# A two-layer image block on one core: how the constants come in, and which engines fold the weights, in its first microseconds

## The chip, the core and the metric

The kernel runs on one core of a Trainium2 chip. A core has five engines that run side by side, each through its own list of instructions in order: TensorE (PE in the profile; its weight loads are PEld), VectorE (DVE), ScalarE (ACT), GpSimd (POOL) and SyncE (SP), which here only starts transfers. Transfers are carried out by 16 DMA engines; an engine that starts one puts it into its own DMA queue. The metric is the device time of one execution in microseconds (us).

## What is computed

The input x is four images of 128 channels by 128 by 128 pixels, in float32. Two layers follow each other, each with a residual:

```
gn(v)    : normalize groups of 4 channels over the whole image
layer 0  : x = x + block(gn(x)) + block(gn(x) transposed, and back)
block(t) : per pixel, over the 128 channels
           t   = ln(t; ln0)
           t   = t + silu(ln(t; ln1)) @ W_out^T
           w   = ln(t; ln2) @ W_whiten^T
           t   = t + sigmoid(w @ W_recep^T) * (relu(w @ W_key^T)^2 @ W_value^T)
layer 1  : x = x + conv3x3(gn(x)) (+ bias), scaled by a gate from channel means
```

The block acts on each pixel by itself, so both calls of layer 0 give the same and the kernel computes it once and counts it twice. Two points matter for what follows. First, gn(x) needs mean and variance of a whole image before its first pixel can be normalized. Second, no nonlinearity stands between W_whiten and W_key or W_recep, so the kernel multiplies these weights with each other once at the start, together with gain and bias of ln2 and with the subtraction of the mean over channels ("folding"). In the loop there is one product with wk_s and bias kbias, and one with wr_s and rbias.

## The kernel before

Channels lie on the 128 partitions. An image is cut into 8 blocks of 16 rows (1 MB each, tiles x) and 32 chunks of 512 pixels; two chunks are a pair, 64 pairs in all. Work on the pairs is software-pipelined: lists of words (FILL, FIRST, ORDER, HANDOVER, END) say by hand, operation by operation, in which order the engines get the steps of different pairs. FILL starts the pipeline; FIRST repeats for image 0 alone; later orders mix in the convolution of layer 1 for the image before. In this hand-ordered part (from line 1010) the order is as written. Before it the scheduler of the tile framework sets the order on each engine; a buffer that is reused is waited for, and so is what an instruction reads.

What comes before the hand-ordered part is what the change touches:

- `load_block` (L284) starts one transfer of a block of x; L292 calls it for the 8 blocks of image 0. The transfers are issued by SP (L287).
- ident, gmat, nhalf and mean_of (L296 to L315) are constants that GpSimd makes. mean_of has 1/128 everywhere.
- `load_const` (L317) issues transfers of constants from ScalarE (L319). `column` (L322) brings a vector of 128 numbers in as a column, one number on each partition: g1, b1, g2, b2, cb. g0 and b0 are read 128 times over, so that each partition holds the whole vector. wo, wv, s1, s2 are weights.
- `times_root` (L325) multiplies the three gains with the square root of 128 on VectorE (L326).
- ww, wkt, wrt (L353) hold W_whiten, W_key and W_recep until they are folded; ScalarE issues them too (L354 to L356).
- The folding loop (L357 to L369) runs twice, for the key weights (512 columns) and the receptance weights (128). TensorE multiplies (pw, L359); VectorE copies to raw (L361) and scales by g2 to raw2 (L362); TensorE makes the column means with mean_of (pc, L364); VectorE subtracts them (L365, into wk_s or wr_s); TensorE multiplies raw with b2 (pb, L368); VectorE copies the bias (L369). L371 halves rbias.
- `in_stats` (L890) takes the statistics of one chunk on VectorE (L894, 32 times for image 0). `input_norm` (L401) runs `group_norm` (L377): VectorE aggregates (mv, L380), TensorE averages over groups (pm L383, pv L391), GpSimd takes the root (L394), and VectorE makes nb (L404).
- Only with nb can `lay` (u, L588, ScalarE) normalize the first chunk, and FILL go on: u is transposed on TensorE (ut), gets its statistics (L601), is normalized to t (L577), and so on.
- `fetch_stats` (L884) loads half-block pieces of later images into a ring of one buffer (xs, L888), for their statistics; SP issues these as well.

Matmul outputs with the tag "h" share two PSUM banks; SBUF tiles with the tag "h" share six buffers, and "y", "y2" and "r" two each.

Of the kernel before, what the change touches and what calls it, by code (L numbers as in the profile page):

```python
# [9 lines left out]
F32 = mybir.dt.float32  # L10
AF = mybir.ActivationFunctionType
ALU = mybir.AluOpType

P = 128
# [3 lines left out]
BLK_ROWS = 16  # L18
# [196 lines left out]
def conv_preact_kernel(  # L215
# [40 lines left out]
    nc = tc.nc  # L256
    B, C, H, W = x.shape
    HID = w_key_t.shape[1]
    NH = HID // P
    NSE = se_w1_t.shape[1]  # L260
    BLK = BLK_ROWS * W
    NBLK = H // BLK_ROWS
# [7 lines left out]
    const = ctx.enter_context(tc.tile_pool(name="const", bufs=1))  # L270
    xp = ctx.enter_context(tc.tile_pool(name="xp", bufs=12))
    wg = ctx.enter_context(tc.tile_pool(name="wg", bufs=4))
    wk = ctx.enter_context(tc.tile_pool(name="wk", bufs=2))
# [5 lines left out]
    def bank(tag, name, bufs=2):  # L279
        return ps.tile([P, CH], F32, tag=tag, name=name, bufs=bufs)  # L280

    blocks = {}

    def load_block(g):  # L284
        b, k = g // NBLK, g % NBLK
        blocks[g] = xp.tile([P, BLK], F32, tag="x", name=f"x_{b}_{k}")
        nc.sync.dma_start(  # L287
            blocks[g],
            x[b, :, k * BLK_ROWS : (k + 1) * BLK_ROWS, :].rearrange("c h w -> c (h w)"),
        )  # L290

    for g in range(NBLK):  # L292
        load_block(g)


    ident = const.tile([P, P], F32, tag="ident", name="ident")  # L296
# [14 lines left out]

    nhalf = const.tile([P, N], F32, tag="nhalf", name="nhalf")
    nc.gpsimd.memset(nhalf, -0.5)
    mean_of = const.tile([P, P], F32, tag="mean_of", name="mean_of")
    nc.gpsimd.memset(mean_of, 1.0 / C)  # L315

    def load_const(name, src, shape):  # L317
        t = const.tile(shape, F32, tag=name, name=name)
        nc.scalar.dma_start(t, src)  # L319
        return t  # L320

    def column(name, src):  # L322
        return load_const(name, src.rearrange("(c o) -> c o", o=1), [P, 1])

    def times_root(t):  # L325
        nc.vector.tensor_scalar(t, t, C**0.5, None, ALU.mult)  # L326

    g1 = column("g1", ln1_g)
    b1 = column("b1", ln1_b)
    g2 = column("g2", ln2_g)  # L330
    b2 = column("b2", ln2_b)
    cb = column("cb", conv_b)
    g0 = load_const("g0", ln0_g.rearrange("(o c) -> o c", o=1).to_broadcast([P, C]), [P, C])
    b0 = load_const("b0", ln0_b.rearrange("(o c) -> o c", o=1).to_broadcast([P, C]), [P, C])
    for gain_of in (g0, g1, g2):
        times_root(gain_of)
    wo = load_const("wo", w_out_t, [P, P])
    wv = load_const("wv", w_value_t.rearrange("(j p) c -> p j c", p=P), [P, NH, P])
    s1 = load_const("s1", se_w1_t, [P, NSE])
    s2 = load_const("s2", se_w2_t, [NSE, P])  # L340

# [1 line left out]
    wk_s = const.tile([P, HID], F32, tag="wk_s", name="wk_s")  # L345
    wr_s = const.tile([P, P], F32, tag="wr_s", name="wr_s")
    kbias = const.tile([P, NH], F32, tag="kbias", name="kbias")
    rbias = const.tile([P, 1], F32, tag="rbias", name="rbias")

    def staged(name, n):  # L350
        return wk.tile([P, n], F32, tag="h", name=name, bufs=6)

    ww, wkt, wrt = staged("ww", P), staged("wkt", HID), staged("wrt", P)  # L353
    nc.scalar.dma_start(ww, w_whiten)  # L354
    nc.scalar.dma_start(wkt, w_key_t)
    nc.scalar.dma_start(wrt, w_recep_t)  # L356
    for src, n, dst, bias in ((wkt, HID, wk_s, kbias), (wrt, P, wr_s, rbias)):  # L357
        pw = bank("h", "pw")
        nc.tensor.matmul(pw[:, :n], ww, src, start=True, stop=True)  # L359
        raw, raw2 = staged("raw", n), staged("raw2", HID)  # L360
        nc.vector.tensor_copy(raw, pw[:, :n])  # L361
        nc.vector.tensor_scalar(raw2[:, :n], raw, g2, None, ALU.mult)  # L362
        pc = bank("h", "pc")
        nc.tensor.matmul(pc[:, :n], mean_of, raw2[:, :n], start=True, stop=True)  # L364
        nc.vector.tensor_tensor(dst, raw2[:, :n], pc[:, :n], ALU.subtract)  # L365
        pb = bank("h", "pb")
        for j in range(n // P):
            nc.tensor.matmul(pb[:, j : j + 1], raw[:, ts(j, P)], b2, start=True, stop=True)  # L368
        nc.vector.tensor_copy(bias, pb[:, : n // P])  # L369

    nc.vector.tensor_scalar(rbias, rbias, 0.5, None, ALU.mult)  # L371


    def col(name):
# [585 lines left out]
    def slot(s, order):  # L960
# [6 lines left out]
        if s % 2 and s + 1 >= NP and len(blocks) < B * NBLK:  # L967
            load_block(len(blocks))
# [26 lines left out]
    def work_off(chain, words, block, pair):  # L995
        for op, n in words:
            if op == "*":
                next(chain, None)
            elif op == "load":
                load_block(len(blocks))  # L1000
            elif op == "fetch":
                fetch_stats(n)
            elif op in ("in0", "in1"):
                in_stats(n, int(op[2]), S["in", n][:, ts(int(op[2]), CH)])
            elif op in EVEN or op in ODD:
                conv_op(op, block(n))
            else:
                layer0_op(op, pair(n))
# [52 lines left out]
```

## Time and profile before

| | |
|---|---|
| median of 8 runs | 1903.68 us (1900.76 to 1907.06) |
| the profiled execution | 1899.84 us |
| its span in the profile | 1898.0 us |
| statistics of image 0 (L894 on x) | 32, mean 681 ns, first at 9.4, last from 37.8 us |
| first instruction of ScalarE on pixels (u, L588) | 42.68 us |
| transfers from ScalarE's queue in the first 40 us | 2288 packets, 0.87 MB |
| transfers from SP's queue in the first 40 us | 1296 packets, 8.91 MB |
| read from HBM, whole run | 97.27 MB |

The profile is one execution, and its span begins with the first instruction. Busy shares on the page are means over the whole span. In a list in order of time, the columns are start, duration, engine, line of the code, operation, tile written and tile read, shape, and the count of instructions merged; in brackets stands how long the engine had stood idle before, and what ended that. A window's row gives, after its length, the busy time of the five engine columns with the count of instructions, the granted clock of TensorE, the share of time in which the 16 DMA engines were busy, and the rate in GB/s.

### The profile page before, as it was taken

Reading aid. Unit: us, or ns where it says so; the run is one execution under the profiler, and the core shown is the slowest. Engines: PE = TensorE matmul, PEld = TensorE weight load, DVE = VectorE, ACT = ScalarE, POOL = GpSimd, SP = SyncE. Lnnn points to the kernel's source line nnn. Section 1 sums busy time; section 2 is a strip of 40 time slices with the busy share of each in tenths; the row PEclk is TensorE's granted clock in tenths of the full one; section 3 lists DMA queues with packets and bytes.
Section 4 is the critical chain, followed back from the end, with each engine's and each line's share of the span. In section 5 each row is a group of like instructions: output and inputs, shape, how many; then the busy total and the mean of one; then the engine's idle time right before and its main releaser. Section 6 shows DMA issues by size and latency. Waiting matters only on the chain.

```text
span 1898.0 us, 21640 instructions
## 1 busy us (share of the span) xinstructions
PE 1810.6 (95%) x6154; PEld 942.7 (50%) x6154; DVE 1359.3 (72%) x3348; ACT 1271.4 (67%) x2478; POOL 1156.8 (61%) x1913
## 2 busy tenths in 40 slices
PE   2699999999999999998999999999999999999998
PEld 1455555555455555454555455455455555554443
DVE  5766776677677677677777677667676667666987
ACT  0789988898667676776777776676577777753000
POOL 0877887897356665665676666666566677631211
PEclk9999999999999999999999999999999999999999
DMA  5311111311122212213222212112111211111112
GB/s 206 89 46 56 56 46 45 124 59 56 56 78 89 89 67 78 78 55 105 72 84 90 69 47 86 67 56 80 47 45 67 67 57 67 49 38 42 53 67 89
DMA packets 41880, 133.68 MB, mean 70 GB/s; under 512 B 5776, under 2 KB 10912, under 8 KB 33568
## 3 DMA queue, kind: packets, MB, share of 16 engines
q1 hardware_dynamic: 39472, 131.42, 19.7%
q10 hardware_dynamic: 2288, 0.87, 0.3%
q8 instruction: 49, 0.80, 0.2%
q14 instruction: 71, 0.58, 0.1%
HBM read 97.27 MB, written 35.00 MB: 70 GB/s over the span
## 4 chain that ended last, share of the span: by engine, by line
PE 84%; DVE 4%; ACT 3%; POOL 3%; issue 1%; DMA 0%; POOLq 0%; DVEq 0%; ACTq 0%
PE kv L735 21%; PE pk L708 21%; PE m L773 8%; PE m L775 8%; PE m L774 8%; PE pr L726 5%; PE att L669 5%; PE tt L570 3%; PE z1t L570 2%; PE ut L570 2%; POOL rs L624 1%; ACT t L577 1%; DVE st L601 1%; ACT z L577 1%; DVE v L797 1%
## 5 line engine op out<-in xcount | busy, mean ns | idle before, releaser
L708 PE MATMUL pk<-y,wk_s 128*128 128x512 f32 x1024 | 500.1, 595 | 7.0 <-DVE y L697 5.6
L735 PE MATMUL kv<-h,wv 128*128 128x512 f32 x1024 | 487.1, 593 | 0.0
L712 ACT ACTIVATE h<-pk,kbias 128x512 f32<-128x512 f32 x512 | 349.9, 686 | 172.0 <-PE pk L708 165.6
L624 POOL TENSOR_TENSOR rs<-rs,nhalf 128x8 f32<-128x8 f32 x192 | 317.4, 1653 | 12.1 <-DVE rs L617 6.0
L735 PEld LDWEIGHTS kv<-h,wv 128*128 128x128 f32 x1024 | 185.9, 190 | 207.5 <-issue 185.8
L718 ACT ACTIVATE h<-h 128x512 f32<-128x512 f32 x480 | 284.5, 630 | 4.2
L708 PEld LDWEIGHTS pk<-y,wk_s 128*128 128x128 f32 x1024 | 182.5, 190 | 195.4 <-issue 146.0
L755 POOL TENSOR_TENSOR x<-x,r 128x512 f32<-128x512 f32 x128 | 164.4, 1285 | 187.8 <-DVE r L751 178.5
L577 ACT ACTIVATE t<-ut,nb,rs 128x128 f32<-128x128 f32 x512 | 191.6, 464 | 125.2 <-POOL nb L631 114.7
L601 DVE BATCH_NORM_STATS2 st<-t 128x6 f32<-128x128 f32 x1024 | 219.5, 276 | 22.1 <-POOL t L652 19.6
L577 ACT ACTIVATE z<-t,nb,rs 128x128 f32<-128x128 f32 x512 | 210.0, 487 | 13.6 <-POOL nb L631 12.8
L648 POOL TENSOR_TENSOR t<-t,g 128x512 f32<-128x512 f32 x128 | 162.9, 1278 | 73.9 <-ACT t L577 73.8
L773 PE MATMUL m<-v,u 128*128 128x512 f32 x384 | 198.8, 599 | 6.7 <-ACT e L849 3.6
L774 PE MATMUL m<-v,u 128*128 128x508 f32 x384 | 194.9, 589 | 0.0
L775 PE MATMUL m<-v,u 128*128 128x508 f32 x384 | 194.9, 589 | 0.0
L613 POOL TENSOR_TENSOR rs<-st 128x8 f32<-128x8 f32 x186 | 57.1, 307 | 210.0 <-DVE st L601 208.4
L652 POOL TENSOR_TENSOR t<-t,b 128x512 f32<-128x512 f32 x128 | 164.0, 1287 | 6.7
L669 PEld LDWEIGHTS att<-wo,y 128*128 128x128 f32 x1024 | 131.1, 196 | 26.2 <-issue 17.8
L601 DVE BATCH_NORM_STATS2 st<-ut 128x6 f32<-128x128 f32 x512 | 112.4, 284 | 41.2 <-PE ut L570 41.2
L730 ACT ACTIVATE r<-pr,rbias 128x512 f32<-128x512 f32 x128 | 87.6, 684 | 80.0 <-PE pr L726 64.7
L669 PE MATMUL att<-wo,y 128*128 128x128 f32 x1024 | 138.4, 280 | 2.2 <-ACT y L663 1.6
L726 PE MATMUL pr<-y,wr_s 128*128 128x512 f32 x256 | 131.7, 597 | 3.2 <-ACT h L712 2.5
(144 smaller groups left out, 2437.3 us busy)
## 6 DMA issues: line engine op xcount, KB each, us to landing
x<-in_x SPq DMA_DIRECT2D x32, 1024.0 KB
R<-rd SPq DMA_DIRECT2D x128, 256.0 KB
out<-x SPq DMA_DIRECT2D x32, 1024.0 KB
xs<-in_x SPq DMA_DIRECT2D x48, 512.0 KB
u<-raw SPq DMA_DIRECT2D x18, 192.0 KB
raw<-u SPq DMA_DIRECT2D x6, 192.0 KB
rd<-rrow SPq DMA_DIRECT2D x64, 4.0 KB
u_w<-in_conv_w SPq DMA_DIRECT2D x3, 192.0 KB
```

The costliest lines, as they stand in the source:

```text
L577: nc.scalar.activation(dst[:, s, :], src[:, s, :], AF.Identity, bias=nb[:, i : i + 1], scale=rs[:, i : i + 1],)
L601: nc.vector.bn_stats(st[:, h * SUB + s, :], src[:, s, :])
L624: nc.gpsimd.tensor_tensor(rs, rs, nhalf, ALU.pow)
L669: nc.tensor.matmul(att[:, ts(s, P)], y[:, ts(s, P)], wo, start=True, stop=True)
L708: nc.tensor.matmul(pk, wk_s[:, ts(j, P)], S["y2", g, h], start=True, stop=True)
L712: nc.scalar.activation(k, S["pk", g, h, j], AF.Relu, bias=kbias[:, j : j + 1])
L718: nc.scalar.activation(k, k, AF.Square)
L726: nc.tensor.matmul(pr, wr_s, S["y2", g, h], start=True, stop=True)
L735: nc.tensor.matmul(S["kv", g, h], wv[:, j, :], S.pop(("h", g, h, j)), start=(j == 0), stop=(j == NH - 1))
L773: nc.tensor.matmul(pc, u[:, 1], v, start=True, stop=False)
L774: nc.tensor.matmul(pc[:, :, 1:W], u[:, 0], v[:, :, 0 : W - 1], start=False, stop=False)
L775: nc.tensor.matmul(pc[:, :, 0 : W - 1], u[:, 2], v[:, :, 1:W], start=False, stop=True)
```

## The change

- Block 7 of image 0, the last of the first eight, is loaded in two halves.
- All constants are issued by SP, in one queue with x, in this order: blocks 0 to 3; the five vectors ln1_g, ln1_b, ln2_g, ln2_b and conv_b as five rows of one tile (vec); ln0_g and ln0_b as one row each; ww, wkt, wrt; blocks 4 to 7; wo, wv, s1, s2.
- The five rows become columns by one matmul with the identity (pv), the two rows are spread over the partitions by a matmul with a row of ones (pr). ScalarE copies them from PSUM and multiplies the gains by the square root of 128 on the way.
- In the folding, ScalarE takes over all that VectorE did. mean_of is replaced by centre, the identity minus 1/128, so that the matmul gives the centred weights and no subtraction is left. The factor 0.5 of rbias is applied with its copy.
- VectorE keeps the statistics alone.

The rest of the kernel, the hand-ordered lists among it, is the same. The core of the diff:

```diff
     def load_block(g):
         b, k = g // NBLK, g % NBLK
         blocks[g] = xp.tile([P, BLK], F32, tag="x", name=f"x_{b}_{k}")
-        nc.sync.dma_start(
-            blocks[g],
-            x[b, :, k * BLK_ROWS : (k + 1) * BLK_ROWS, :].rearrange("c h w -> c (h w)"),
-        )
-
-    for g in range(NBLK):
+        parts = 2 if g == NBLK - 1 else 1
+        R = BLK_ROWS // parts
+        for i in range(parts):
+            r = k * BLK_ROWS + i * R
+            nc.sync.dma_start(
+                blocks[g][:, i * R * W : (i + 1) * R * W],
+                x[b, :, r : r + R, :].rearrange("c h w -> c (h w)"),
+            )
+
+    def load_const(name, src, shape, pool=const, tag=None):
+        t = pool.tile(shape, F32, tag=tag or name, name=name)
+        nc.sync.dma_start(t, src)
+        return t
+
+    def staged(name, n, src=None):
+        t = wk.tile([P, n], F32, tag="h", name=name, bufs=6)
+        if src is not None:
+            nc.sync.dma_start(t, src)
+        return t
+
+    for g in range(NBLK // 2):
         load_block(g)
+    vec = wk.tile([5, C], F32, tag="y", name="vec")
+    for i, src in enumerate((ln1_g, ln1_b, ln2_g, ln2_b, conv_b)):
+        nc.sync.dma_start(vec[i : i + 1, :], src.rearrange("(o c) -> o c", o=1))
+    row0 = [
+        load_const(n, src.rearrange("(o c) -> o c", o=1), [1, C], wk, "y2")
+        for n, src in (("g0row", ln0_g), ("b0row", ln0_b))
+    ]
+    ww, wkt = staged("ww", P, w_whiten), staged("wkt", HID, w_key_t)
+    wrt = staged("wrt", P, w_recep_t)
+    for g in range(NBLK // 2, NBLK):
+        load_block(g)
+    wo = load_const("wo", w_out_t, [P, P])
+    wv = load_const("wv", w_value_t.rearrange("(j p) c -> p j c", p=P), [P, NH, P])
+    s1 = load_const("s1", se_w1_t, [P, NSE])
+    s2 = load_const("s2", se_w2_t, [NSE, P])
...
-    mean_of = const.tile([P, P], F32, tag="mean_of", name="mean_of")
-    nc.gpsimd.memset(mean_of, 1.0 / C)
-
-    def load_const(name, src, shape):
-        t = const.tile(shape, F32, tag=name, name=name)
-        nc.scalar.dma_start(t, src)
-        return t
-
-    def column(name, src):
-        return load_const(name, src.rearrange("(c o) -> c o", o=1), [P, 1])
-
-    def times_root(t):
-        nc.vector.tensor_scalar(t, t, C**0.5, None, ALU.mult)
...
+    centre = staged("centre", P)
+    nc.gpsimd.memset(centre, -1.0 / C)
+    nc.gpsimd.tensor_tensor(centre, centre, ident, ALU.add)
+    ones = wk.tile([1, P], F32, tag="r", name="ones")
+    nc.gpsimd.memset(ones, 1.0)
+
+    pv = bank("h", "pvec")
+    nc.tensor.matmul(pv[:, :5], vec, ident[:5, :5], start=True, stop=True)
+    columns = []
+    for i, (name, by) in enumerate((("g1", C**0.5), ("b1", 1.0), ("g2", C**0.5), ("b2", 1.0), ("cb", 1.0))):
+        t = const.tile([P, 1], F32, tag=name, name=name)
+        nc.scalar.mul(t, pv[:, i : i + 1], by)
+        columns.append(t)
+    g1, b1, g2, b2, cb = columns
+    rows0 = []
+    for name, row, by in (("g0", row0[0], C**0.5), ("b0", row0[1], 1.0)):
+        pr = bank("h", "prow")
+        nc.tensor.matmul(pr[:, :C], ones, row, start=True, stop=True)
+        t = const.tile([P, C], F32, tag=name, name=name)
+        nc.scalar.mul(t, pr[:, :C], by)
+        rows0.append(t)
+    g0, b0 = rows0
...
-    for src, n, dst, bias in ((wkt, HID, wk_s, kbias), (wrt, P, wr_s, rbias)):
+    for src, n, dst, bias, by in ((wkt, HID, wk_s, kbias, 1.0), (wrt, P, wr_s, rbias, 0.5)):
         pw = bank("h", "pw")
         nc.tensor.matmul(pw[:, :n], ww, src, start=True, stop=True)
         raw, raw2 = staged("raw", n), staged("raw2", HID)
-        nc.vector.tensor_copy(raw, pw[:, :n])
-        nc.vector.tensor_scalar(raw2[:, :n], raw, g2, None, ALU.mult)
+        nc.scalar.activation(raw2[:, :n], pw[:, :n], AF.Identity, scale=g2)
+        nc.scalar.copy(raw, pw[:, :n])
         pc = bank("h", "pc")
-        nc.tensor.matmul(pc[:, :n], mean_of, raw2[:, :n], start=True, stop=True)
-        nc.vector.tensor_tensor(dst, raw2[:, :n], pc[:, :n], ALU.subtract)
+        nc.tensor.matmul(pc[:, :n], centre, raw2[:, :n], start=True, stop=True)
+        nc.scalar.copy(dst, pc[:, :n])
         pb = bank("h", "pb")
         for j in range(n // P):
             nc.tensor.matmul(pb[:, j : j + 1], raw[:, ts(j, P)], b2, start=True, stop=True)
-        nc.vector.tensor_copy(bias, pb[:, : n // P])
-
-    nc.vector.tensor_scalar(rbias, rbias, 0.5, None, ALU.mult)
+        nc.scalar.mul(bias, pb[:, : n // P], by)
```

More of the change, by code (lines that the diff above doesn't have):

```diff
@@ L313, in conv_preact_kernel @@
     nc.gpsimd.memset(nhalf, -0.5)
-    mean_of = const.tile([P, P], F32, tag="mean_of", name="mean_of")
-    nc.gpsimd.memset(mean_of, 1.0 / C)
-    def load_const(name, src, shape):
-        t = const.tile(shape, F32, tag=name, name=name)
-        nc.scalar.dma_start(t, src)
-        return t
-    def column(name, src):
-        return load_const(name, src.rearrange("(c o) -> c o", o=1), [P, 1])
-    def times_root(t):
[L326 to L340, printed above, removed]
+    centre = staged("centre", P)
[19 more added lines that the diff above has]
+    g0, b0 = rows0
     wk_s = const.tile([P, HID], F32, tag="wk_s", name="wk_s")
@@ L348, in conv_preact_kernel @@
     rbias = const.tile([P, 1], F32, tag="rbias", name="rbias")
[L350 to L356, printed above, removed]
-    for src, n, dst, bias in ((wkt, HID, wk_s, kbias), (wrt, P, wr_s, rbias)):
+    for src, n, dst, bias, by in ((wkt, HID, wk_s, kbias, 1.0), (wrt, P, wr_s, rbias, 0.5)):
         pw = bank("h", "pw")
```

## The prediction

> **What bounds the kernel now.** I read the page first, then the time-ordered list of VectorE for the first 50 us, the one-microsecond windows of the same stretch, the waits of the first 43 us, and last the windows of the later stages. From the page:
>
> ```profile
> PE 1810.6 (95%) x6154; PEld 942.7 (50%) x6154; DVE 1359.3 (72%) x3348; ACT 1271.4 (67%) x2478; POOL 1156.8 (61%) x1913
> PE   2699999999999999998999999999999999999998
> PE 84%; DVE 4%; ACT 3%; POOL 3%; issue 1%; DMA 0%; POOLq 0%; DVEq 0%; ACTq 0%
> ```
>
> TensorE is busy 95% of the span, and the chain that ended last is 84% TensorE. But one slice in 40 is 47 us, and the first shows PE at 2 tenths: there is a start in which TensorE has little to do. The chain reaches back to 70.5 us only. What lies before has to be read from the list of VectorE's instructions (start, duration, instruction, idle time before it and what ended it):
>
> ```profile
> 9.26 0.23 DVE L326 TENSOR_SCALAR g<-g 128x128 f32<-128x128 f32 x1 [2.53 <-DMA g<-in_ln_g]
> 9.40 2.47 DVE L894 BATCH_NORM_STATS2 st<-x 128x6 f32<-128x512 f32 x4
> 14.82 2.47 DVE L894 BATCH_NORM_STATS2 st<-x 128x6 f32<-128x512 f32 x4 [2.96 <-DMA x<-in_x]
> 18.95 0.69 DVE L894 BATCH_NORM_STATS2 st<-x 128x6 f32<-128x512 f32 x1 [1.66 <-DMA x<-in_x]
> 23.78 0.69 DVE L365 TENSOR_TENSOR wk_s<-raw,pc 128x512 f32<-128x512 f32 x1 [1.03 <-PE pc L364]
> 28.91 9.58 DVE L894 BATCH_NORM_STATS2 st<-x 128x6 f32<-128x512 f32 x16
> 38.52 1.02 DVE L380 BATCH_NORM_AGGREGATE mv<-st 128x2 f32<-128x192 f32 x1
> 42.49 0.16 DVE L404 SCALAR_TENSOR_TENSOR nb<-mg,rs 128x1 f32<-128x1 f32 x1 [0.75 <-POOL rs L394]
> ```
>
> The reader should see that the statistics of image 0 (32 instructions L894) end at 38.5 us, that half of them run after 28.9 us without a gap, and that they came late for three reasons: VectorE first waited for the gains (to 9.26), then for blocks 1 and 2 of x, and then did the folding (L361 to L371) between them. Everything hangs on it:
>
> ```profile
> ACT u L588 <- DVE nb L404: 26.2, 1, 26.2
> PE pm L383 <- DVE mv L380: 11.6, 1, 11.6
> ```
>
> The windows (length, PE, PEld, DVE, ACT, POOL busy, clock, DMA share, GB/s) say why x was late:
>
> ```profile
> 4.00:5.00 1.00, 0.00 (x0) 0.00 (x0) 0.00 (x0) 0.00 (x0) 0.00 (x0) 1.00 1.01 402
> 7.00:8.00 1.00, 0.00 (x0) 0.00 (x0) 0.00 (x0) 0.00 (x0) 0.00 (x0) 1.00 0.63 34
> 12.00:13.00 1.00, 0.00 (x0) 0.00 (x0) 0.00 (x0) 0.00 (x0) 0.00 (x0) 1.00 1.06 370
> 32.00:33.00 1.00, 0.00 (x0) 0.00 (x0) 1.00 (x2) 0.00 (x0) 0.00 (x0) 1.00 0.03 12
> ```
>
> From 5 to 9 us only 34 to 59 GB/s move. SP has issued one block then; its next issue stands at 6.17 us and the one after at 11.91, and SP's own waits put 5.4 and 5.0 us on the vectors b and g of ScalarE's queue. The image is on the chip by 32 us at the latest. The later stages:
>
> ```profile
> 50.00:60.00 10.00, 2.23 (x8) 1.43 (x8) 7.54 (x34) 4.46 (x12) 7.95 (x6) 1.00 0.31 100
> 80.00:90.00 10.00, 8.49 (x35) 5.18 (x34) 8.80 (x27) 8.17 (x18) 9.00 (x16) 0.88 0.36 107
> 120.00:160.00 40.00, 40.00 (x158) 22.32 (x157) 27.96 (x75) 35.24 (x70) 29.60 (x51) 1.00 0.20 63
> 600.00:1000.00 400.00, 392.55 (x1347) 203.63 (x1346) 295.77 (x722) 282.96 (x549) 256.26 (x423) 1.00 0.22 77
> ```
>
> From 42 to 86 us a chain of short dependent steps runs, and from about 86 us TensorE is full. Both begin from nb (L404); neither waits for anything fixed in time. In 42 to 90 us the only wait on a transfer is 1.8 us of VectorE for xs.
>
> **What the skill says.** "DMA: Bandwidth & Descriptors", Rules for kernel authors: a transfer whose last dimension isn't contiguous becomes one descriptor per element. The trace agrees: 1,136 packets under 512 B in the first 40 us, and the drop to 34 GB/s. Same page, Issuing engines are not separate DMA queues: several issuing engines share the same 16 engines, so a second queue brings no bandwidth. The trace agrees: 419 GB/s from 15 to 30 us, 98.6% of DMA time in SP's queue alone. "ScalarE: Activation LUTs", Table sets: copy and identity are in every set. The trace agrees: after Silu's table load (65.22 us, 1.28 us) Identity runs without another. "TensorE: Matmul & The Clock Gate", What's actually happening: the clock is released by a free-running window of about 3.4 us. Here a group of four ut transposes takes 1.12 us at 62.2 and 0.66 us at 72.7, so the phase can move the warm-up.
>
> **The change, step by step.** The sum is made on the profiled execution: span 1898.0, its time 1899.84 us, 1.84 more. The median shown, 1903.68, is 3.84 above it; I subtract the gain from the median.
>
> 1. The image's arrival. Removed: five columns of 4-byte elements, two vectors spread over 128 partitions, and ScalarE's queue. The 13 transfers of the latter move behind blocks 0 to 3 on SP. SP issues at 0.33 to 0.45 us each; with the split block it has 23 issues before the first xs (L888), some 10 us in all, while it needs 20 us to move the image: issue is hidden. Bytes moved by 5 us are 90+180+328+402 KB, 1.0 MB, so block 0 is there at about 5.5 us (nothing mixed in before that but its 4-byte packets). Then seven blocks of 1,049 KB at 419 GB/s: 7 x 2.50 = 17.5. In front of block 4 lie 384 KiB of weights; with small rows mixed in (10 to 14 us) 361 to 390 GB/s moved: 1.05 us. Seven rows of 512 B: by bytes 0.01 us. Counted in bytes, the last half block is in at 5.1 + 17.5 + 1.05 = 23.7. Landing lags the count: in before, three blocks and most of ScalarE's queue are counted in at about 17.2 us, VectorE got block 2 at 18.95, up to 1.75 us late; block 0 lags about 0.5. I take 0.6 at the end of the stream, 24.3 us; bounds 23.9 to 25.5.
>
> 2. VectorE. Removed: three L326 (0.53 us), two L361 (0.97), two L362 (0.74), two L365 (0.98), two L369 and L371 (0.46), 3.7 us, with their waits. What stays are 32 statistics at 0.60 us (9.58/16), 19.2 us. From 5.6 us they could end at 24.8 at the soonest; a block takes 2.4 of the 2.5 us it takes to arrive, so VectorE keeps up and ends two instructions (1.28) after the last half: 25.6 us. The half block saves 1.2 us here against a whole one. So the aggregation L380 starts at 25.6 instead of 38.52: gain 12.9 us. Bounds: 24.8 (13.7) and 26.8 (11.7).
>
> 3. Folding on PE and ScalarE. Vectors land at about 13.5 us (5.5 + three blocks + 0.5), weights at about 14.3. Durations of ScalarE from the kernel's own rows: 128x1 0.169 (L509), 128x128 0.277 (L506), 128x512 Identity 0.697 (L849), copy 0.586 (L851); cold matmuls from before: pw and pc 2.04, pb 1.71 for eight, the small ones 0.78, 0.77, 0.43. Columns and rows: 5 x 0.2 + 2 x (0.4 + 0.3) + waits on two banks, to about 15.5. Then pw 17.5, scaled copy 18.2, pc 20.3, copy 20.9, pb 22.0, bias 22.2, pw 22.8, 23.1, pc 23.9, 24.2, bias 24.5. TensorE needs pm at 25.6 + 1.02 = 26.6: hidden by 2 us. ScalarE work, some 5 us, lies in its 26.2 us of idle time. Without that cover each microsecond late costs one. GpSimd's ones and centre replace mean_of (0.2 us) in a GpSimd idle for 39 us: nothing. The table load moves to ScalarE's first use, in idle time too.
>
> 4. wo, wv, s1, s2 now follow the image: 0.4 MB, 1 us, and xs 16 after them, on the chip by 28 us; first needed by VectorE at 47.46 - 12.9 = 34.6 and by att at 54. Hidden.
>
> 5. From 26 us on the same instructions run in the same order, 12.9 us sooner; what is late next is the same chain from L380, now behind the arrival of x. The warm-up's phase may give or take 1.5 us.
>
> Sum: 1899.84 - 12.9 = 1886.9 on the profile, 1903.7 - 12.9 = 1890.8 on the median. Own range of this case 1888 to 1894.
>
> **Rivals.**
> - Folding becomes late. Fourteen microseconds of dependent steps behind transfers on one queue; if these land 3 us late or ScalarE's order holds one bank, pm waits behind pb on TensorE. For: only 2 us of slack. Against: every duration is known. Price 2 to 7 us: 1893 to 1898, say 1895.
> - More comes out: VectorE's 1.8 us wait for xs goes and the warm-up falls well: 15 us, 1888. For: xs is fetched long before. Against: later xs fetches follow the ring's buffer, not the clock.
> - The gain is eaten in the hand-ordered fill (42 to 86 us): about 1902, no change. Against: nothing in it is fixed in time.
> - Slower: each one-row transfer sits on one DMA engine, and that engine holds back its rows of blocks 4 to 7 until the row is confirmed. Seven rows at t us put image arrival back by 7t; beyond t = 1.84 the gain is gone, at 3 us the time is 1903.7 - 12.9 + 21 = 1911.8. No one-row transfer in before is timed. Against: between blocks, where each engine also confirms, the windows stay at 397 to 434 GB/s.
>
> **Numbers.** Forecast 0.73, folding late 0.12, more 0.05, eaten 0.05, slower 0.05. So 1890.8 us; the range 1887 to 1897 holds the first three but for their tails. A change is told from none beyond 0.2% (3.8 us): faster 0.90, within 0.05, slower 0.05.
>
> **What would show it.** Right: L380 near 25.6 us, DMA above 400 GB/s from 4 to 24 us without a hole, L894 in groups of four with short waits on x, the last wr_s and rbias before pm, ScalarE's first u near 29.8, TensorE full from about 73. Wrong: a hole in the rate after block 3, pm waiting for anything but mv, or L404 early and TensorE's full stage not.

## The result, and the profile after

| | before | after |
|---|---|---|
| median | 1904.2 us (30 runs) | 1895.68 us (11 runs, 1891.73 to 1897.84) |
| ratio of the times | | 0.9958, 95% interval 0.9949 to 0.9966 |
| span of the profiled execution | 1898.0 us | 1889.9 us |
| aggregation of image 0's statistics starts | 38.52 us (L380) | 30.78 us (L400) |
| nb, on which all else waits | 42.49 us (L404) | 34.72 us (L424) |
| first product with the folded weights (pk) | 85.69 us | 77.66 us |

The change saves 0.42%, 8.0 us (0.0042 x 1904.2); 12.9 us were forecast. Two of the 30 runs of before took 3923 and 8420 us, and the ratio is formed without such slow runs. The lower rows show where it lies: nb comes 7.77 us sooner, pk 8.03 us, the end 8.1 us. Nothing of the gain is lost after nb; what is missing was never gained before it. From the page after, the busy time and the chain that ended last:

```profile
PE 1811.1 (96%) x6160; PEld 942.7 (50%) x6160; DVE 1355.8 (72%) x3336; ACT 1276.2 (68%) x2493; POOL 1157.9 (61%) x1915
PE 86%; DVE 4%; ACT 4%; POOL 3%; issue 1%; POOLq 0%; DVEq 0%; ACTq 0%
```

TensorE has the same work as before in a shorter span. VectorE's list in order of time, after (start, duration, instruction, idle before and what ended it):

```profile
5.54 9.91 DVE L914 BATCH_NORM_STATS2 st<-x 128x6 f32<-128x512 f32 x16 [5.54 <-DMA x<-in_x]
20.89 9.85 DVE L914 BATCH_NORM_STATS2 st<-x 128x6 f32<-128x512 f32 x16 [5.44 <-DMA x<-in_x]
30.78 1.02 DVE L400 BATCH_NORM_AGGREGATE mv<-st 128x2 f32<-128x192 f32 x1
34.72 0.16 DVE L424 SCALAR_TENSOR_TENSOR nb<-mg,rs 128x1 f32<-128x1 f32 x1 [0.68 <-POOL rs L414]
```

VectorE now does two runs of 16 statistics without a gap, and between them stands idle for 5.44 us, until block 4 lands. The windows of one microsecond (last two columns: DMA share and GB/s) show that this isn't the bandwidth:

```profile
11.00:12.00 1.00, 0.00 (x0) 0.00 (x0) 1.00 (x3) 0.00 (x0) 0.00 (x0) 1.00 1.00 426
12.00:13.00 1.00, 0.00 (x0) 0.00 (x0) 1.00 (x3) 0.00 (x0) 0.00 (x0) 1.00 0.16 61
13.00:14.00 1.00, 0.29 (x2) 0.32 (x2) 1.00 (x2) 0.00 (x0) 0.00 (x0) 1.00 0.01 3
16.00:17.00 1.00, 0.75 (x1) 0.50 (x2) 0.00 (x0) 0.00 (x0) 0.00 (x0) 1.00 0.49 156
```

From 12.1 to 14.3 us there is next to nothing to carry. Why, is in SP's own list, the issue of transfers:

```profile
0.79 2.09 SPq L291 DMA_DIRECT2D x<-in_x  x4
2.92 0.34 SPq L313 DMA_DIRECT2D vec<-in_ln_g  x1
...
3.88 0.25 SPq L313 DMA_DIRECT2D vec<-in_ln_b  x1
5.53 0.22 SPq L313 DMA_DIRECT2D vec<-in_conv_b  x1
8.01 0.22 SPq L298 DMA_DIRECT2D g0row<-in_ln_g  x1
10.51 0.22 SPq L298 DMA_DIRECT2D b0row<-in_ln_b  x1
12.98 0.36 SPq L304 DMA_DIRECT2D ww<-in_w_whiten  x1
...
14.32 3.64 SPq L291 DMA_DIRECT2D x<-in_x  x5
```

Eight transfers go out at once: four blocks, four rows. The ninth waits to 5.53 us and the next three go 2.5 us apart, which is the pace at which blocks land (VectorE got block 0 at 5.54). Each of the last three rows, 512 bytes, waited for a block of a megabyte, and behind the rows waited the weights and block 4. SP's waits name the same releaser:

```profile
SPq L298 <- DMA x<-in_x: 5.3, 3, 2.3
SPq L304 <- DMA x<-in_x: 2.2, 1, 2.2
SPq L313 <- DMA x<-in_x: 1.4, 1, 1.4
```

"Perfetto Trace Analysis", DMA Instruction — HWDGE, in the Trainium skill says how to read such a list: the profiler's start of an issuing instruction is the moment at which its semaphores are satisfied. The trace agrees: the late issues last 0.22 us like any other row's, the wait stands before them. A semaphore is a counter that a transfer raises as it lands, and for which an instruction can wait.

The trace also keeps, for each issuing instruction, the semaphore on which its transfer is counted and the one for which it waits. SP's transfers use eight semaphores in turn (100, 101, 103 to 108), and from the ninth on each issuing instruction waits for the very semaphore on which its own transfer will count. So the ninth waits until the first has landed, the tenth until the second has, and so on. The eight is therefore written into the instructions of this program; it need not be a limit of the DMA engines.

### The profile page after: what moved, and what is told of

Same layout as the page of the kernel before. It is cut to its first block, busy times and chain, and to the rows that moved or that the text cites. A ratio compares the mean times of both kernels' runs of the same rounds, so it can differ in the third digit from the quotient of the medians.

```text
span 1889.9 us, 21666 instructions
## 1 busy us (share of the span) xinstructions
PE 1811.1 (96%) x6160; PEld 942.7 (50%) x6160; DVE 1355.8 (72%) x3336; ACT 1276.2 (68%) x2493; POOL 1157.9 (61%) x1915
## 4 chain that ended last, share of the span: by engine, by line
PE 86%; DVE 4%; ACT 4%; POOL 3%; issue 1%; POOLq 0%; DVEq 0%; ACTq 0%
PE kv L755 21%; PE pk L728 21%; PE m L793 8%; PE m L795 8%; PE m L794 8%; PE pr L746 5%; PE att L689 5%; PE tt L590 3%; PE ut L590 2%; PE z1t L590 2%; ACT t L597 1%; POOL rs L644 1%; DVE st L621 1%; ACT z L597 1%; ACT h L732 1%
## 5 line engine op out<-in xcount | busy, mean ns | idle before, releaser
L644 POOL TENSOR_TENSOR rs<-rs,nhalf 128x8 f32<-128x8 f32 x192 | 316.9, 1651 | 11.8 <-DVE rs L637 6.0
```

Of the source, the lines that this page charges most:

```text
L644: nc.gpsimd.tensor_tensor(rs, rs, nhalf, ALU.pow)
```

## The experiments

Two theories of the hole. A: at most eight transfers are in flight; each waits for the one eight places before it in the order of issue. B: the one-row transfers cost by themselves, on SP's queue or on a DMA engine (the prediction's rival on the slow side). Changes of time below are 1 minus the ratio, times the median of before beside it.

**Rows between the blocks.** The same transfers, same queue, other order (in short; x7 is two halves):

```diff
-    x0 x1 x2 x3  row row row row row row row  ww wkt wrt  x4 x5 x6 x7
+    x0 x1 row x2 row x3 row row x4 row row row  ww wkt wrt  x5 x6 x7
```

> The changed kernel, with the same 24 transfers on the same queue in another order: x0 x1 row x2 row x3 row row x4 row row row ww wkt wrt x5 x6 x7a x7b. Theory A (eight transfers are in flight at most: each is issued only when the one eight places before it has landed; four rows behind four blocks used up the eight, so the queue ran dry at 12 us): with the blocks spread among the rows there is no hole, DMA stays above 300 GB/s from 3 to 24 us, the aggregation starts at 26.3 to 27.0 us instead of 30.8, and the time is about 4 us below the changed kernel, ratio to before 0.993 to 0.995. Theory B (each one-row transfer holds a DMA engine or SP's queue for about half a microsecond by itself): seven rows cost the same 3.6 us wherever they stand, aggregation at 30 us or later, ratio 0.995 to 0.997.

Ratio 0.9942 (0.9929 to 0.9956), 11.0 us below before. VectorE's list of this kernel:

```profile
5.63 12.53 DVE L925 BATCH_NORM_STATS2 st<-x 128x6 f32<-128x512 f32 x20 [5.63 <-DMA x<-in_x]
19.22 7.35 DVE L925 BATCH_NORM_STATS2 st<-x 128x6 f32<-128x512 f32 x12 [1.06 <-DMA x<-in_x]
26.60 1.02 DVE L411 BATCH_NORM_AGGREGATE mv<-st 128x2 f32<-128x192 f32 x1
```

and its window over the place of the hole, where the changed kernel moved 69 GB/s:

```profile
12.00:15.00 3.00, 0.00 (x0) 0.00 (x0) 2.99 (x6) 0.00 (x0) 0.00 (x0) 1.00 1.00 413
```

The hole is gone, with all seven rows still there: B falls, A stands. The packets in the trace of the changed kernel agree: the seven rows were carried one behind the other from 12.22 to 12.43 us, 27 ns each, and their landings came 0.18 us apart. The aggregation comes 4.18 us sooner than in the changed kernel.

**Rows on ScalarE's queue.** The seven one-row transfers issued by ScalarE:

```diff
-        nc.sync.dma_start(vec[i : i + 1, :], src.rearrange("(o c) -> o c", o=1))
+        nc.scalar.dma_start(vec[i : i + 1, :], src.rearrange("(o c) -> o c", o=1))
```

(the same for g0row and b0row)

> The changed kernel with its seven one-row transfers issued from ScalarE, all else on SP as it is. Theory A in its stricter form (the eight places are shared by all queues): the hole stays, SP issues ww near 13 us, aggregation at 30 to 31.5 us, ratio 0.995 to 0.997. Theory A with eight places to each queue, or theory B (the rows hold SP's queue): SP goes on from block 3 to ww at once, no hole, aggregation at 26.3 to 27.0 us, ratio 0.993 to 0.995.

Neither: ratio 0.9955 (0.994 to 0.9969), aggregation at 29.14 us. SP's list:

```profile
0.79 0.38 SPq L291 DMA_DIRECT2D x<-in_x  x1
...
2.03 0.33 SPq L291 DMA_DIRECT2D x<-in_x  x1
...
5.67 0.33 SPq L291 DMA_DIRECT2D x<-in_x  x1
```

and ScalarE's:

```profile
0.78 0.51 ACTq L313 DMA_DIRECT2D vec<-in_ln_g  x1
...
2.76 0.27 ACTq L317 DMA_DIRECT2D b0row<-in_ln_b  x1
```

ScalarE sends its seven rows from 0.78 us on, beside block 0. Together these are eight, and they hold the eight semaphores. Block 1 has the ninth place, and waits for the first row:

```profile
SPq L291 <- DMA vec<-in_ln_g: 0.8, 1, 0.8
```

SP issues it at 2.03 us, as that row has landed; block 2 waits for block 0 and goes at 5.67. At 2.03 us only five transfers had been issued, so it isn't their number that held block 1 back, but the one semaphore: "eight in flight" is a loose name for "each waits for the one eight places before it". The hole has moved forward: VectorE waited 1.07, 1.48 and 1.08 us for blocks 1, 2 and 4. What I had expected of the place of the hole was wrong, since I had counted in the order of the source and not in that in which the semaphores are given out, with the rows of ScalarE next to block 0; the rule itself, eight over both queues, is what explains the list.

**Block 7 whole.** `parts = 1` for all blocks.

> The changed kernel with block 7 loaded whole. By the prediction's working the half saves 1.2 us, so the aggregation comes 1.2 us later, at 32.0. By the trace of the changed kernel VectorE is busy without a gap from the landing of block 4 on (16 statistics in 9.85 us) and is a block behind when block 7 lands, so the aggregation moves by less than 0.3 us and the ratio stays at 0.9958 within 0.001.

Ratio 0.9964 (0.9952 to 0.9976). VectorE's list:

```profile
21.69 9.99 DVE L914 BATCH_NORM_STATS2 st<-x 128x6 f32<-128x512 f32 x16 [5.97 <-DMA x<-in_x]
31.72 1.02 DVE L400 BATCH_NORM_AGGREGATE mv<-st 128x2 f32<-128x192 f32 x1
```

The aggregation is 0.94 us later than in the changed kernel, more than the 0.3 I had allowed. But of that, 0.80 us stands before the last 16 statistics: block 4 landed at 21.69 instead of 20.89. The 16 themselves run without a gap in both, 9.99 and 9.85 us: the half block saves 0.14 us there, not 1.2. Of the 0.80 us, 0.26 are there when block 4 is issued (14.58 instead of 14.32 us). Why the rest came (the rate from 15 to 21 us was 284 GB/s, 325 in the changed kernel) stays open.

**The two parts alone.** Loads, rows and matmuls of the change, with copies and folding on VectorE (each nc.scalar.mul, copy and activation of the folding becomes its nc.vector form):

> One part of the change alone: transfers, rows and matmuls as in the changed kernel, but VectorE makes all copies from PSUM and the folding, as before. If VectorE's folding adds to the statistics in full, 3.7 us plus waits of up to 2: aggregation at 34.5 to 36.5, ratio 0.997 to 0.999. If half of it falls into the 5.4 us in which VectorE waits for block 4: aggregation at 32 to 33.5 us, ratio 0.9965 to 0.9975.

And the reverse: transfers as before, gains scaled and weights folded on ScalarE with centre:

> The other part of the change alone: transfers as before (columns and spread vectors on ScalarE's queue), but the gains are scaled and the weights folded on ScalarE and with centre. Block 2 of x lands at 18.9 us as before; from there 24 statistics at 0.61 us without folding between them, so the aggregation starts at 33.6 to 34.5 us instead of 38.5 if the rest of x keeps coming at 2.5 us a block, ratio 0.9973 to 0.998. If the folding on VectorE had only filled gaps, it stays above 37 us and the ratio above 0.999.

Loads alone: 0.9973 (0.9966 to 0.9981), 5.1 us; VectorE's list:

```profile
21.39 0.69 DVE L914 BATCH_NORM_STATS2 st<-x 128x6 f32<-128x512 f32 x1 [1.40 <-DMA x<-in_x]
...
33.94 1.02 DVE L400 BATCH_NORM_AGGREGATE mv<-st 128x2 f32<-128x192 f32 x1
```

Folding alone: 0.9979 (0.997 to 0.9988), 4.0 us; VectorE's list:

```profile
20.77 12.54 DVE L893 BATCH_NORM_STATS2 st<-x 128x6 f32<-128x512 f32 x20 [2.37 <-DMA x<-in_x]
33.34 1.02 DVE L379 BATCH_NORM_AGGREGATE mv<-st 128x2 f32<-128x192 f32 x1
```

Each part moves the aggregation by about 5 us (4.6 and 5.2), both together by 7.7. In the loads alone, part of the folding falls into the wait for block 4, where it costs nothing; the aggregation at 33.94 lies between my two cases. In the folding alone, block 3 is late (20.77 us), since ScalarE's many small transfers are still in the order (SP waited 9.1 us for wo before it); from there VectorE runs through. The places of the transfers had shifted here, though their code is that of before: block 1 came at 13.17 us and not at 14.82, and block 3 landed 0.9 us sooner than in before. So not all of the 5.2 us is VectorE's own work. Taking work off VectorE while its data come late, and bringing data sooner while VectorE folds, each leave the other's wait.

**All blocks in halves, rows and weights between them, and the same with the weights last.** The diff between the two:

```diff
-    ww, wkt = staged("ww", P, w_whiten), staged("wkt", HID, w_key_t)
-    wrt = staged("wrt", P, w_recep_t)
     for g in range(4, NBLK):
         load_half(g, 0)
         load_half(g, 1)
+    ww, wkt = staged("ww", P, w_whiten), staged("wkt", HID, w_key_t)
+    wrt = staged("wrt", P, w_recep_t)
```

> The changed kernel with all eight blocks in halves and the rows, then the weights, between them so that the transfer eight places before has always landed in time. By theory A (eight in flight) there is no hole; VectorE starts at 3.5 to 4 us instead of 5.5, and is half a block behind at the end instead of a whole one, so the aggregation starts at 25.0 to 25.7 us, 1 us before the kernel with rows between whole blocks, and the time is 5 us below the changed kernel, ratio 0.9925 to 0.994. If every further transfer costs by itself, the 32 transfers bring it to 27 us or later.

> The same, with ww, wkt and wrt behind block 7. The order on TensorE is the same, folding ahead of pm. The image is in 1 us earlier, so the aggregation starts at 24.3 to 25 us; but the folding takes 8.6 us from wkt's landing (as in the changed kernel, 16.2 to 24.8), starts near 25, and pm waits behind it: pm at 33 to 34.5 us, nb at 36 to 37, the time 6 to 8 us above the kernel with the weights ahead, ratio 0.9965 to 0.9975. If pm doesn't wait, the time is 1 us below that kernel.

Halves: 0.9938 (0.9923 to 0.9953), aggregation at 28.49, not 25.0 to 25.7. Weights last: 0.9972 (0.9962 to 0.9981). Its VectorE and then its TensorE list:

```profile
27.27 1.02 DVE L423 BATCH_NORM_AGGREGATE mv<-st 128x2 f32<-128x192 f32 x1
36.23 0.16 DVE L429 COPY mg<-pm 128x1 f32<-128x1 f32 x1 [7.94 <-PE pm L426]
```

```profile
26.91 2.04 PE L404 MATMUL pw<-wkt,ww 128*128 128x512 f32 x2 [12.73 <-DMA wkt<-in_w_key_t]
...
35.61 0.58 PE L426 MATMUL pm<-mv,gmat 128*128 128x1 f32 x2
```

This is the prediction's rival of a late folding, made on purpose: 8.7 us pass from pw to pm, pm waits on TensorE behind products that it doesn't need, and VectorE waits 7.94 us. The time is 6.5 us above that with the weights ahead (0.0034 x 1903.18), as expected; the single stages came later than expected (aggregation at 27.27, pm at 35.61, nb at 38.41). In the changed kernel this rival had no part: the last folding product is done at 24.8 us, pm starts at 31.94.

That the time of the halves lies in its expected range, with an aggregation 3 us late, is partly luck: the time is lower by 11.8 us, with 3 us of uncertainty to each side, while nb came only 10.1 us sooner. The missing gain of the halves is in the rates. From 15 to 21 us, in the kernel with all halves and in that with rows between whole blocks (its second run), in this order:

```profile
15.00:21.00 6.00, 5.13 (x12) 2.55 (x12) 3.08 (x6) 1.75 (x3) 0.00 (x0) 1.00 0.97 351
```

```profile
15.00:21.00 6.00, 4.45 (x9) 2.42 (x10) 4.63 (x8) 2.14 (x9) 0.00 (x0) 1.00 1.03 413
```

The DMA engines are nearly as busy, but the halves move 351 GB/s where the whole blocks move 413. From 3 to 12 us the same halves had moved 404, and from 20 to 26 us they moved 399. What slows them in between is open. The trace shows this much: each such transfer is counted by sixteen updates of its semaphore, and for the first half of block 4 these came spread from 15.98 to 17.77 us; for block 5 in the kernel with rows between whole blocks they lay within 0.4 us in the first run and 0.6 in the second.

**Fewer halves, and both kernels again on one chip.** Blocks 0, 5, 6 and 7 in halves, in the order with rows between the blocks, from which the diff is taken:

```diff
-        parts = 2 if g == NBLK - 1 else 1
+        parts = 2 if g in (0, 5, 6, 7) else 1
...
     vec_row(2)
-    vec_row(3)
     load_block(4)
+    vec_row(3)
     vec_row(4)
```

> The kernel with rows between blocks (aggregation at 26.6 us), with blocks 0, 5, 6 and 7 in halves. If what bounds it now is the landing of block 5 and then VectorE a whole block behind, VectorE starts at 4 us, begins block 5 half a block sooner, and the aggregation comes at 25.3 to 26.0 us, ratio 0.9932 to 0.9945. If halves are carried more slowly (350 GB/s instead of 410, as between 14 and 21 us with all blocks in halves), the aggregation comes at 26.6 us or later and nothing is gained.

> The kernel with rows between whole blocks once more, on the same chip as the changed kernel: aggregation at 26.6 us as before, 4.2 us ahead of the changed kernel's, and a time 3 to 4 us below it.

> The changed kernel itself, for that comparison: ratio to before 0.995 to 0.9966, aggregation at 30.5 to 31.5 us.

Fewer halves: 0.9948 (0.9935 to 0.9961), aggregation at 27.90 us. Its SP list:

```profile
14.35 0.43 SPq L304 DMA_DIRECT2D wrt<-in_w_recep_t  x1
16.51 2.79 SPq L291 DMA_DIRECT2D x<-in_x  x6
```

Here I fell into the same trap myself. Counted in places, the first half of block 5 is now the eighth after block 4, so it waited for block 4's landing, and from 15 to 21 us 271 GB/s moved. It is one more witness for A. Once past that wait, from 20 to 26 us, this kernel too carried halves:

```profile
20.00:26.00 6.00, 4.67 (x15) 3.33 (x15) 5.87 (x10) 2.44 (x6) 0.00 (x0) 1.00 1.02 406
```

At 406 GB/s, halves aren't slow as such.

Rows between, again: 0.9939 (0.9924 to 0.9953), median 1890.56 us; the changed kernel on the same chip: 0.9965 (0.9952 to 0.9977), median 1896.44. Aggregation at 26.88 and 30.70. So an order of transfers alone is worth another 3 to 5 us (11.0 less 8.0, and 11.6 less 6.7 on one chip, where 3 to 4 had been expected). The kernel with rows between whole blocks beats the changed kernel; its lead over the one with fewer halves, 1.7 us, is within the uncertainty.

All runs beside each other, against nb in before (42.49 us):

| kernel | nb, us | nb sooner by | time lower by (1 - ratio) |
|---|---|---|---|
| folding alone | 37.28 | 5.2 | 4.0 |
| loads alone | 37.76 | 4.7 | 5.1 |
| weights last | 38.41 | 4.1 | 5.3 |
| block 7 whole | 35.67 | 6.8 | 6.8 |
| the change; again | 34.72; 34.65 | 7.8; 7.8 | 8.0; 6.7 |
| rows on ScalarE | 33.08 | 9.4 | 8.6 |
| fewer halves | 31.84 | 10.7 | 9.9 |
| all halves | 32.44 | 10.1 | 11.8 |
| rows between; again | 30.54; 30.82 | 12.0; 11.7 | 11.0; 11.6 |

The time follows nb within 1.8 us in every row; the intervals of the ratios are some 1 to 3 us to each side.

## Why the prediction was right, and where its size was off

Direction and mechanism held: the start was bound by the statistics of image 0, the change brings them sooner, and from nb on the rest moves as a block. The time, 1895.68 us, lies in the range of 1887 to 1897, but not in that of the main case, 1888 to 1894. That the wider range held it is partly luck: it had been drawn to take in the late folding, which had no part. Of the signs of being wrong that the prediction names, one came true, the hole in the rate after block 3. The gain was 8.0 us and not 12.9, and the aggregation came at 30.78 and not 25.6 us, outside its bounds of 24.8 to 26.8. Two terms of the sum make up the 5.2 us.

- Step 1, the image's arrival: "it has 23 issues before the first xs (L888), some 10 us in all, while it needs 20 us to move the image: issue is hidden." I had counted the duration of issues, not the wait before them, and took 24.3 us for the last landing. From the ninth transfer on, each issue waits for a landing. By its last semaphore update the last half block landed at 28.73 us; with the hole filled by order alone, it landed at 24.34 and 24.76, so the count of bytes was right and the wait was left out. The aggregation then came at 26.60 and 26.88: the hole is 4 us of the 5.2 (30.78 and 30.70 less these). The trace of before had held the hint: SP's second block was issued at 6.17 us, and SP's waits named ScalarE's vectors:

```profile
SPq L287 <- DMA b<-in_ln_b: 5.4, 1, 5.4
SPq L287 <- DMA g<-in_ln_g: 5.0, 1, 5.0
```

I laid that to the 4-byte columns, and so thought that it would go with them. It was the same rule: the seven vectors and block 0 held the eight semaphores, block 1 waited for the first column (landed at 6.15 us) and block 2 for the last spread vector (11.89). How much of the low rate from 5 to 9 us was the small packets, and how much that no block was issued, the runs don't separate. (ScalarE's queue in before has 14 transfers, not 13; the sum doesn't rest on it.)

- Step 2, VectorE: "VectorE keeps up and ends two instructions (1.28) after the last half: 25.6 us. The half block saves 1.2 us here". Without a hole the aggregation is still at 26.6 to 26.9, 1.0 to 1.3 us above 25.6. A block can be started only when it has landed, and then takes 2.46 us. Blocks land at about the same pace, so VectorE has only begun block 7 when its last half lands: the aggregation came 2.05 us after that landing (30.78 less 28.73), and 2.26 and 2.12 us after it with rows between the blocks, not 1.28. With the block whole, the last 16 statistics took 9.99 us instead of 9.85: the half saves 0.14.

Right by its numbers: step 3, the folding. Forecast were vectors at 13.5, last bias at 24.5; measured 13.7 (pvec starts) and 25.0 (rbias done), and pm didn't wait for it. The weights were late, though: wkt landed at 16.1 us, not 14.3, because their issue waited too. It cost little, since the forecast had given TensorE the columns and rows until 15.5 us anyway; pw began at 16.25. With the hole gone, pm still came 1.6 and 2.0 us after the last folding product, near the 2 us forecast. That this cover matters was shown with the weights last. Step 4 (the later constants hidden): xs is read at 39.69 us without a wait. Step 5: passed on in full, 7.8 us at nb and 8.0 in the time.

The rivals: a late folding had no part in the changed kernel, where pm did not wait for it; more than forecast and eaten in the fill didn't happen; rows that hold a DMA engine fell with the rows between the blocks, which left all seven in place and lost the hole, and with the landings of the rows, 0.18 us apart where 1.84 us each would have eaten the gain. What I had described as the slower rival, blocks 4 to 7 behind seven rows, was nearest to what took place, for another reason: places in the order of semaphores, not engines.

## What to carry to other kernels

Count the places of transfers, not only their bytes and issue times: here each transfer waited for the one eight places before it, over both queues, so a row of 512 bytes could hold up what stood behind it for as long as the megabyte it waited for. Put small transfers between large ones, so that the eight places always hold enough bytes. VectorE worked here through blocks at the pace at which they land; it ended almost a whole block late, and cutting the last block hardly helped. And when work is taken off a late engine, ask first whether its data will be there.

## What the runs showed that I had not expected

- Eight semaphores for all transfers of SP and ScalarE together, each transfer waiting for the one eight places before it: the change, rows on ScalarE, fewer halves, rows between, and before itself fit it to the instruction. The wait stands in the issuing instructions; no run here had another number of semaphores.
- In one kernel half blocks were carried at 351 GB/s from 15 to 21 us, where another carried whole ones at 413, with the DMA engines nearly equally busy; from 20 to 26 us halves moved at 399 and 406. The loss has a place in time, and its cause is open.
- One kernel's profiled executions differ, and so does their granted clock: rows between had a span of 1892.8 us at 0.993 and 1888.1 at 0.996. Apart from the first table, whose two executions both had 0.996, single spans are therefore not compared above, but stages and ratios.
